# Expert tiles in a pinned order, gathers several tiles ahead, and one gathered row per expert in layer 2

## The chip, the cores and the metric

The kernel runs on one core of a Trainium2 chip, as one launch. The metric is the device time of a run in microseconds; lower is better. A core has five engines with their own instruction streams: PE (TensorE, matrix products into PSUM), DVE (VectorE), ACT (ScalarE), POOL (GpSimd) and SP (SyncE). SP and ACT issue plain DMAs, POOL issues the gathers by index. An engine works through its own stream in order and waits on semaphores for the others.

## The reference

Four layers work on x of 8 sequences with 256 tokens of 256 numbers (2048 tokens in all). Each layer is a cross attention with 16 heads of 16 on ctx_1024, then a feed-forward block, each behind a layer norm and added to x with a gate:

```python
x = x + tanh(g_xattn[i]) * xattn_i(layernorm(x), ctx_1024)
x = x + tanh(g_ffn[i])   * ffn_i(layernorm(x))
```

Layers 1 and 2 have a mixture of experts as their feed-forward block, and the change is about these. Each token picks 2 of 8 experts; hidden size H is 1024 in layer 1 and 512 in layer 2:

```python
w, ind = top_k(x_flat @ Wr, 2)             # 2 of 8 experts per token
w = softmax(w, axis=-1)
# for each expert e, with ce its weight per token (0 where it was not picked):
h = gelu(x_flat @ W1[e] + b1[e])           # [tokens, H]
out += ce[:, None] * (h @ W2[e] + b2[e])   # [tokens, 256]
```

Layer 2 normalises its tokens by their root mean square first and adds its own input again. Layer 0's feed-forward block is a plain one, layer 3's one with ternary weights and a convolution. All products of the experts are in float32.

## The kernel before

`moe(l, ...)` is run between two attention stages, once for layer 1 and once for layer 2. `route` (from line 773) finds the two experts of each token. `slots` (from line 813) sorts the 4096 pairs of token and expert by expert, each expert's share rounded up to whole tiles of 128: `NTL` = 39 tiles. It leaves two index tables: `toki`, which token stands in each row of each tile, and `wrow`, which rows of the weight tables a tile needs.

`experts` (from line 950) then works tile by tile. The 39 tiles are cut into `WSETS` = 3 runs of `PER` = 13 consecutive tiles. Each run has its own weight buffers ("a set"), and `order` takes one tile of each run in turn. Where a tile has the same expert as the tile before it in its run, `slots` has put an index out of bounds into `wrow`: the gather is still issued, but moves no weights (lines 869 to 879). Per tile j there are three steps:

- `fetch(j)`: three gathers on POOL (line 944): 128 token rows from `xd` into `xg`, then the first weights with b1 (`w1e`), then the second weights with b2 (`w2e`). The loop calls it two tiles ahead.
- `first(j)`: two transposes of the tokens (`ptg`, line 978), their copy into `xgT` on DVE (line 981, or 983 with the norm's weights), 16 products in layer 1 or 8 in layer 2 (`phg`, line 994), and as many Gelus on ACT (`hg`, line 1000).
- `second(j)`: 8 or 4 products of 256 columns (`yg`, line 1009), the sum with b2 on DVE (`ysb`, line 1014), and the write to `yd` in DRAM by SP (line 1015).

The loop runs `first(order[k])`, `second(order[k - 1])`, then pieces of the next stage whose place is at most k (`early`), then `fetch(order[k + 2])`. This order is not what the engines see: the tile framework orders each engine's stream itself, by priority and by its own estimate of when things are ready. Only instructions that were given to `pin` (line 132) keep their order among each other on their engine. `mm` and `turn` (lines 174 and 179) are pinned forms of a product and a transpose; the attention stages use them. The expert products before the change were not pinned.

`early` holds work of the next attention stage that needs no tokens: `setup(l)` (weights and bias of that layer), and the K and V projections of its first two jobs (`EARLY` = 2; a job is one sequence of one layer). Each job has four such steps, `proj("k", 0)`, `proj("k", 1)`, `vals(0)` and `vals(1)`, and `stack` cuts K into three bf16 parts, writes them to DRAM (`dr_k`) and reads them back in seven row groups by six DMAs into `kstack`, all on SP. In layer 2's stage `early` also holds the ternary weights of layer 3 (sums on DVE, `wsum` on PE).

After the stage, `element(b)` of `experts` gathers the results of a sequence (`yg<-yd`, four gathers on POOL per sequence) and adds them to x on DVE (line 1047). Then the attention's `norm` (with a pow on POOL, line 154), `normT` and the Q projection follow.

`ones_of` (line 198) fills what is constant in a K stack and a V buffer: rows 96 to 127 of the stack are set to 1 (rows 112 to 114 are used so, the others are overwritten), and the V buffer gets its column of ones. The stacks of jobs 0 and 1 live through the whole kernel, the third belongs to each attention's own pool and is filled anew in each of the three runs, by POOL (line 199).

Of the kernel before, what the change touches and what calls it, by code (L numbers as in the profile page):

```python
# [8 lines left out]
F32 = mybir.dt.float32  # L9
BF16 = mybir.dt.bfloat16  # L10
I32 = mybir.dt.int32
AF = mybir.ActivationFunctionType
ALU = mybir.AluOpType
AX = mybir.AxisListType

P = 128
B, S, D = 8, 256, 256
# [3 lines left out]
DC = D // P  # L21
# [3 lines left out]
NE = 8  # L25
NTL = 2 * T // P + NE - 1
NEG = -(2.0**100)
WSETS = 3
PER = -(-NTL // WSETS)
EARLY = 2  # L30
# [8 lines left out]
def kernel(ctx: ExitStack, tc: tile.TileContext, a: dict, out: bass.AP):  # L39
# [157 lines left out]

    def ones_of(engine, ks, va):
        engine.memset(ks[96:P], 1.0)
        engine.memset(va[:, :, :, DK : DK + 1], 1.0)  # L200
        engine.memset(va[:, :, :, DK + 1 :], 0.0)

    def attention(layers):
# [61 lines left out]
        def prep(j, l, b):  # L265
# [4 lines left out]
            def begin():  # L270
                if j < 3 and (j >= EARLY or l == 0):
                    ones_of(nc.vector if j < EARLY else nc.gpsimd, stacks["k"][j], vas[j])
                o["nm"] = pool.tile([P, 2, NH], F32, tag="nm", name=f"nm_{n}", bufs=3)

            def context():
# [105 lines left out]
            def vals(i):  # L381
# [9 lines left out]
                )  # L391

            if l == 0:
                return [
                    (-3, begin), (-3, context), (-2, norm), (3, normT), (4, contextT), (5, biasT),
                    (6, contextV),
                ]
# [4 lines left out]
            if j < EARLY:  # L402
                early.extend([(NTL - 11 + 4 * j + i, f) for i, (_, f) in enumerate(kv)])
                kv = []
            return [
                (-6, begin), (-5, norm), (0, normT),
# [405 lines left out]

    def slots(l, pool, scratch, one1, one2):

# [33 lines left out]
        while k < NE:  # L848
# [6 lines left out]

        n = WSETS * PER
        ge = tmp("ge", [P, n, NE])
# [10 lines left out]

        ts = te.rearrange("p (w i) -> p w i", w=WSETS)
        same = tmp("same", [P, WSETS, PER - 1])  # L870
        nc.vector.tensor_tensor(same, ts[:, :, 1:], ts[:, :, : PER - 1], ALU.is_equal)
        wr = tmp("wr", [P, n])
        nc.vector.tensor_copy(wr, te)
        nc.vector.scalar_tensor_tensor(
            wr.rearrange("p (w i) -> p w i", w=WSETS)[:, :, 1:], same, float(NE * P),
            ts[:, :, 1:], ALU.mult, ALU.add,
# [72 lines left out]

    def experts(l, pool, xd, chosen, rows, nh, scale, early):  # L950
        one1, one2, wa, wb = chosen
        toki, wrow, s1, s2 = rows
        yd = dram.tile([NTL * P, D], F32, name=f"yd{l}")
        n1 = DC * nh * P
        xg, w1, w2, hs = {}, {}, {}, {}
        wsets = [
            (
                pool.tile([P, n1 + nh], F32, tag=f"w1e{k}", name=f"w1e{l}_{k}", bufs=1),
                pool.tile([P, nh * D + D], F32, tag=f"w2e{k}", name=f"w2e{l}_{k}", bufs=1),
            )  # L960
            for k in range(WSETS)
        ]

        def fetch(j):
            xg[j] = pool.tile([P, D], F32, tag="xg", name=f"xg{l}_{j}", bufs=4)
            gather(xg[j], xd[:, :], toki[:, j : j + 1])
            w1[j], w2[j] = wsets[j // PER]
            for w, n in ((w1[j], "a"), (w2[j], "b")):
                gather(
                    w, a[f"L{l}_ffn_w{n}"], wrow[:, j : j + 1],  # L970
                    bounds_check=NE * P - 1, oob_is_err=False,
                )

        def first(j):
            pv = bank(ps_m, "m", f"ptg{l}_{j}")[:, : DC * P].rearrange("p (c s) -> p c s", c=DC)
            x_ = xg.pop(j)
            for c in range(DC):
                nc.tensor.transpose(pv[:, c, :], x_[:, c * P : (c + 1) * P], ident)
            xT = pool.tile([P, DC, P], F32, tag="xgT", name=f"xgT{l}_{j}", bufs=2)
            if scale is None:  # L980
                nc.vector.tensor_copy(xT, pv)
            else:
                nc.vector.tensor_tensor(
                    xT, pv, scale[:, :, None].to_broadcast([P, DC, P]), ALU.mult
                )
            h = pool.tile([P, nh, P], F32, tag="hg", name=f"hg{l}_{j}", bufs=2)
            w = w1[j]
            for g in range(nh // 4):
                ph = bank(ps_s, "s", f"phg{l}_{j}_{g}").rearrange("p (k s) -> p k s", k=4)
                for k in range(4):  # L990
                    hc = 4 * g + k
                    for c in range(DC):
                        lo = c * nh * P + hc * P
                        nc.tensor.matmul(  # L994
                            ph[:, k, :], lhsT=w[:, lo : lo + P], rhs=xT[:, c, :],
                            start=(c == 0), stop=(c == DC - 1),
                        )
                for k in range(4):
                    hc = 4 * g + k
                    nc.scalar.activation(  # L1000
                        h[:, hc, :], ph[:, k, :], AF.Gelu, bias=w[:, n1 + hc : n1 + hc + 1]
                    )
            hs[j] = h

        def second(j):
            py = bank(ps_t, "t", f"yg{l}_{j}")[:, :D]
            h = hs.pop(j)
            for hc in range(nh):
                nc.tensor.matmul(  # L1009
                    py, lhsT=h[:, hc, :], rhs=w2[j][:, hc * D : (hc + 1) * D],  # L1010
                    start=(hc == 0), stop=(hc == nh - 1),
                )
            ys = pool.tile([P, D], F32, tag="ysb", name=f"ysb{l}_{j}", bufs=3)
            nc.vector.tensor_tensor(ys, py, w2[j][:, nh * D :], ALU.add)  # L1014
            nc.sync.dma_start(yd[j * P : (j + 1) * P, :], ys)

        order = [
            j for i in range(PER) for j in range(i, WSETS * PER, PER) if j < NTL
        ]
        for j in order[:2]:  # L1020
            fetch(j)

        early = sorted(early, key=lambda q: q[0])
        for k in range(NTL + 1):
            if k < NTL:
                first(order[k])
            if k:
                second(order[k - 1])
            while early and early[0][0] <= k:
                early.pop(0)[1]()  # L1030
            if k + 2 < NTL:
                fetch(order[k + 2])

        def element(b):
            rows = [
                (t, s, w) for t in (2 * b, 2 * b + 1) for s, w in ((s1, wa), (s2, wb))
            ]
            g = []

            def fetched(pool):  # L1040
                for k, (t, s, w) in enumerate(rows):
                    g.append(pool.tile([P, D], F32, tag="yg", name=f"yg{l}_{b}_{k}", bufs=4))
                    gather(g[k], yd[:, :], s[:, t : t + 1])

            def added(pool):
                for k, (t, s, w) in enumerate(rows):
                    pin(nc.vector.scalar_tensor_tensor(
                        x[t], g[k], w[:, t, :], x[t], ALU.mult, ALU.add
                    ))

            at = NH * (b - 2) - AHEAD
            return [(at - 16, fetched), (at - 7, added)]

        return [q for b in range(B) for q in element(b)]
# [209 lines left out]

    def moe(l, nh, lg, xd, gate, early, scale=None):
        with tc.tile_pool(name=f"c{l}", bufs=1) as pool:
            with tc.tile_pool(name=f"rt{l}", bufs=1) as tmp:
                chosen = route(pool, tmp, lg, gate, l)
                rows = slots(l, pool, tmp, chosen[0], chosen[1])
            with tc.tile_pool(name=f"f{l}", bufs=1) as tiles:  # L1270
                return experts(l, tiles, xd, chosen, rows, nh, scale, early)

# [6 lines left out]
    early, run = attention((2,))  # L1279
    ahead = moe(1, 8, lg[0], xd[0], tg[:, 5:6], early)  # L1280
    with tc.tile_pool(name="r2", bufs=2) as pool:
# [3 lines left out]
    with tc.tile_pool(name="f3w", bufs=1) as home:  # L1285
        weights, pieces = ffn3(home)
        ahead = moe(2, 4, lg[1], xd[1], tg[:, 6:7], early + weights, w["nw"])
        with tc.tile_pool(name="r3", bufs=2) as pool:
            run(pool, pieces(pool), ahead)


def _layout(inputs):
# [43 lines left out]
    for l, w1, w2 in (  # L1336
# [5 lines left out]
        b1 = g[f"L{l}_ffn_b1"].reshape(NE, -1, P).transpose(0, 2, 1).reshape(NE * P, -1)  # L1342
        r[f"L{l}_ffn_wa"] = np.concatenate([first, b1], axis=1)

        second = w2.reshape(NE, -1, P, D).transpose(0, 2, 1, 3).reshape(NE * P, -1)
        b2 = np.repeat(g[f"L{l}_ffn_b2"], P, axis=0)
        r[f"L{l}_ffn_wb"] = np.concatenate([second, b2], axis=1)
    r["L3_ffn_w1"], r["L3_ffn_w2"] = g["L3_ffn_w1"].T, g["L3_ffn_w2"].T
# [26 lines left out]
```

## Time and profile before

| | us |
|---|---|
| median of 3 runs | 1856.42 (1855.35 to 1860.22) |
| profiled execution | 1884.49, its span 1882.7 |
| layer 1's expert stage, first gather to last output | 624.8 to 925.0 |
| layer 2's expert stage, first gather to last output | 1233.8 to 1434.3 |

The profile shows one execution. Busy times in it count an engine's instructions; a product in float32 has two records on PE and two on PEld (loading of the stationary operand). A row of the timeline has the start, the length, the engine, the line, the operation and the tiles it writes and reads; what stands in brackets is how long the engine had been idle and what ended that. "issue" there means that the profile shows no cause. The kernel has 27329 instructions, of which PE has 9856 products; PE is busy in 77% of the span, DVE in 49%, ACT in 39%, POOL in 38%. The mean granted clock of PE is 0.893 of full speed.

### The profile page before, as it was taken

How to read it: one execution, taken by the hardware profiler on the slowest of the kernel's cores; microseconds unless marked ns; L12 is line 12 of the kernel's file. 1: busy time of each engine (PE TensorE's matmuls, PEld its weight loads, DVE VectorE, ACT ScalarE, POOL GpSimd, SP SyncE). 2: the span in 40 equal slices, each digit the busy share in tenths (PEclk: the TensorE clock that was granted, in tenths of full speed). 3: DMA queues.
4: the chain of work that ended last, by engine and by line, in shares of the span. 5: the costliest groups of instructions: out<-in, count | busy, mean ns of one | idle time of the engine just before them, and what ended most of it. 6: DMA issues, size and time to landing. Idle time of an engine off the chain costs nothing.

```text
span 1882.7 us, 27329 instructions
## 1 busy us (share of the span) xinstructions
PE 1447.0 (77%) x9856; PEld 1093.2 (58%) x9886; DVE 921.1 (49%) x2642; ACT 739.8 (39%) x1623; POOL 723.5 (38%) x849
## 2 busy tenths in 40 slices
PE   1598898989996699999658978458885667667753
PEld 1366666766664599999635655347784345444422
DVE  5655554345564210112155676522222557778877
ACT  0255454545553133233214545112221246555641
POOL 4342322232310433434344541055654534544352
PEclk9999999999997799999868999779997688888876
DMA  8653222324440432325236443133443452222000
GB/s 213 136 125 73 63 57 57 75 67 86 110 100 29 168 107 68 124 88 148 69 87 133 118 101 82 62 113 103 133 129 79 103 106 68 68 63 67 9 6 17
DMA packets 101981, 170.02 MB, mean 90 GB/s; under 512 B 30355, under 2 KB 84502, under 8 KB 92118
## 3 DMA queue, kind: packets, MB, share of 16 engines
q1 hardware_dynamic: 68096, 114.33, 24.8%
q0 software_dynamic: 29280, 52.83, 10.0%
q10 hardware_dynamic: 4470, 1.10, 0.3%
q8 instruction: 79, 1.29, 0.3%
q14 instruction: 56, 0.46, 0.1%
HBM read 224.69 MB, written 41.68 MB: 141 GB/s over the span
## 4 chain that ended last, share of the span: by engine, by line
PE 52%; DVE 16%; DMA 10%; issue 10%; POOL 7%; ACT 3%; SPq 1%; ACTq 0%; POOLq 0%; another core or an unknown queue 0%; DVEq 0%
PE yg L1009 10%; PE phg L994 10%; PE y_f L175 4%; PE po L175 4%; PE ph_f L175 4%; PE st L175 3%; PE sc L175 3%; PE pq L175 3%; DMA kstack<-dr_k 3%; DMA qstack<-dr_q 3%; PE pk L175 2%; DVE nm L432 2%; PE pv L175 2%; DVE h_f L1188 1%; DVE ms L427 1%
## 5 line engine op out<-in xcount | busy, mean ns | idle before, releaser
L476 ACT ACTIVATE pT<-st 128x512 f32<-128x512 f32 x512 | 298.4, 597 | 288.8 <-PE st L175 232.5
L432 DVE TENSOR_REDUCE nm<-sc 128x2 f32<-128x512 f32 x384 | 257.2, 684 | 152.6 <-PE sc L175 151.1
L175 PE MATMUL sc<-kstack,qstack 112*128 112x256 bf16 x1024 | 214.4, 295 | 115.5 <-DMA kstack<-dr_k 25.8
L1000 ACT ACTIVATE hg<-phg,w1e 128x128 f32<-128x128 f32 x468 | 133.8, 369 | 308.2 <-issue 230.3
L1009 PE MATMUL yg<-w2e,hg 128*128 128x256 f32 x936 | 228.9, 386 | 24.3 <-ACT hg L1000 14.4
L994 PEld LDWEIGHTS phg<-xgT,w1e 128*128 128x128 f32 x1872 | 225.3, 196 | 14.1 <-issue 7.9
L994 PE MATMUL phg<-xgT,w1e 128*128 128x128 f32 x1872 | 227.3, 279 | 7.2 <-DMA w1e<-in_L_ffn_wa,sl_wrow 5.6
L175 PE MATMUL st<-qstack,kstack 115*128 115x256 bf16 x1024 | 208.0, 288 | 29.5 <-ACT pT L476 26.8
L175 PEld LDWEIGHTS <-qstack 112*128 112x128 bf16 x1024 | 100.8, 104 | 185.7 <-issue 108.4
L1009 PEld LDWEIGHTS yg<-w2e,hg 128*128 128x128 f32 x936 | 169.2, 192 | 49.0 <-ACT hg L1000 19.9
L1014 DVE TENSOR_TENSOR ysb<-yg,w2e 128x256 f32<-128x256 f32 x78 | 33.1, 424 | 328.1 <-PE yg L1009 297.3
L175 PE MATMUL po<-pT,va 128*32 128x256 f32 x2048 | 151.5, 413 | 0.9
L427 DVE CUSTOM_DVE_ANT_0 ms<-sc,mb 128x256 f32<-128x256 f32 x256 | 107.5, 420 | 77.9 <-PE sc L175 67.7
L944 POOL DMA_INDIRECT w2e<-in_L_ffn_wb,sl_wrow x78 | 77.3, 991 | 163.7 <-DVE ysb L1014 155.9
L175 PEld LDWEIGHTS <-kstack 115*128 115x128 bf16 x1024 | 104.5, 103 | 56.6 <-issue 37.3
L154 POOL TENSOR_TENSOR rsr_ff<-rsv_ff,nhalf 128x4 f32<-128x4 f32 (+2 forms) x24 | 24.4, 1017 | 227.4 <-DVE rsv_ff L152 123.9
L944 POOL DMA_INDIRECT xg<-xd,sl_toki x78 | 77.1, 988 | 89.5 <-DVE sl_toki L940 65.9
L944 POOL DMA_INDIRECT w1e<-in_L_ffn_wa,sl_wrow x78 | 77.5, 993 | 54.3 <-ACT hg L1000 32.7
L944 POOL DMA_INDIRECT yg<-yd,sl_si x64 | 62.8, 981 | 81.9 <-issue 39.6
L175 PEld LDWEIGHTS po<-pT,va 128*32 128x32 f32 x2048 | 56.5, 114 | 60.9 <-issue 37.7
L184 POOL CAST pc_q<-qT 128x512 bf16<-128x512 f32 x22 | 14.4, 654 | 176.0 <-ACT qT L371 133.1
L180 PE MATMUL px<-ident,xn 128*128 128x128 f32 x128 | 26.9, 346 | 68.9 <-DVE xn L330 68.7
(253 smaller groups left out, 2486.8 us busy)
## 6 DMA issues: line engine op xcount, KB each, us to landing
kstack<-dr_k SPq DMA_DIRECT2D x160, 128.0 KB
qstack<-dr_q SPq DMA_DIRECT2D x64, 256.0 KB
dr_q<-pc_q SPq DMA_DIRECT2D x32, 384.0 KB
dr_k<-pc_k SPq DMA_DIRECT2D x32, 384.0 KB
qstack<-dr_q SPq DMA_DIRECT2D x32, 384.0 KB
yd<-ysb SPq DMA_DIRECT2D x78, 128.0 KB
kstack<-dr_k SPq DMA_DIRECT2D x32, 256.0 KB
xd<-fxn_f SPq DMA_DIRECT2D x8, 512.0 KB
```

Source lines behind the costliest of these rows:

```text
L154: nc.gpsimd.tensor_tensor(rs, ve, nhalf[:, :k, :n], ALU.pow)
L175: pin(nc.tensor.matmul(out, lhsT=lhsT, rhs=rhs, start=start, stop=stop, skip_group_check=True))
L180: pin(nc.tensor.transpose(out, in_, idn))
L427: nc.vector.tensor_tensor_reduce(masked, sc[:, i, :], o["bias"][:, i, :], -1.0, 3.0e38, ALU.add, ALU.min, o["nm"][:, i, h : h + 1],)
L432: nm = nc.vector.tensor_reduce(o["nm"][:, :, h], sc, AX.X, ALU.max, negate=True)
L476: pin(nc.scalar.activation(pT[u], st, AF.Exp))
L944: return nc.gpsimd.indirect_dma_start(out=dst, out_offset=None, in_=src, in_offset=bass.IndirectOffsetOnAxis(ap=rows, axis=0), **kw,)
L994: nc.tensor.matmul(ph[:, k, :], lhsT=w[:, lo : lo + P], rhs=xT[:, c, :], start=(c == 0), stop=(c == DC - 1),)
L1000: nc.scalar.activation(h[:, hc, :], ph[:, k, :], AF.Gelu, bias=w[:, n1 + hc : n1 + hc + 1])
L1009: nc.tensor.matmul(py, lhsT=h[:, hc, :], rhs=w2[j][:, hc * D : (hc + 1) * D], start=(hc == 0), stop=(hc == nh - 1),)
L1014: nc.vector.tensor_tensor(ys, py, w2[j][:, nh * D :], ALU.add)
L1188: nc.vector.scalar_tensor_tensor(y, hp[:, k, t : t + S], cw[:, hc, t : t + 1], y, ALU.mult, ALU.add)
```

## The change

The expert stage is rewritten:

- Transposes and products go through `turn` and `mm`, and the gathers of tokens and weights through `pin`. PE's order is then that of the program: products of tile k, transposes of tile k+1, second products of tile k-1.
- Tokens are gathered four tiles ahead (five buffers instead of four). The weights of the next tile of the same set are gathered as soon as the code has passed the last use of the buffer: in layer 1 the first weights behind `first(k)`, the second behind `second(k - 1)`; in layer 2 both in one gather behind `second(k - 1)`.
- Layer 1 keeps three sets and two gathers per tile (`apart`). Layer 2 gets five sets, and its four weight parts lie in one row of one table (2308 numbers), fetched by one gather per tile. The table is laid out on the host as before.
- The early K and V projections: those of job 0 are placed at k = 32 to 35 (28 to 31 before), those of job 1 all at k = 39, behind the last tile (32 to 35 before).
- The third K stack is no longer filled by a memset on POOL: a DMA on SP copies the three rows of ones out of job 0's stack. The V buffer's memsets stay on POOL.

```diff
+            def ones_own():
+
+                nc.sync.dma_start(stacks["k"][j][NR : NR + 3], kkeep[0][NR : NR + 3])
+                ones_of(nc.gpsimd, vas[j])
...
+            own = [(0, ones_own)] if j == EARLY else []
...
-                early.extend([(NTL - 11 + 4 * j + i, f) for i, (_, f) in enumerate(kv)])
+                early.extend([(NTL - 7 + i if j == 0 else NTL, f) for i, (_, f) in enumerate(kv)])
...
-        n = WSETS * PER
+        per = -(-NTL // nsets)
+        n = nsets * per
...
-    def experts(l, pool, xd, chosen, rows, nh, scale, early):
+    def experts(l, pool, xd, chosen, rows, nh, scale, early, nsets, apart):
...
+        cuts = [(0, n1), (n1, n1 + n2)] if apart else [(0, n1 + n2)]
...
+        def tokens(k):
+            if k < NTL:
+                j = order[k]
+                xg[j] = pool.tile([P, D], F32, tag="xg", name=f"xg{l}_{j}", bufs=5)
+                pin(gather(xg[j], xd[:, :], toki[:, j : j + 1]))
+
+        def weights(k, part):
+
+            if k < NTL and part < len(cuts):
+                j = order[k]
+                lo, hi = cuts[part]
+                pin(gather(
+                    wsets[j // per][:, lo:hi], a[f"L{l}_ffn_w{'ab'[part] if apart else ''}"],
+                    wrow[:, j : j + 1], bounds_check=NE * P - 1, oob_is_err=False,
+                ))
+
+        def turns(k):
...
-                nc.tensor.transpose(pv[:, c, :], x_[:, c * P : (c + 1) * P], ident)
+                turn(pv[:, c, :], x_[:, c * P : (c + 1) * P], ident)
...
-                        nc.tensor.matmul(
-                            ph[:, k, :], lhsT=w[:, lo : lo + P], rhs=xT[:, c, :],
-                            start=(c == 0), stop=(c == DC - 1),
-                        )
+                        mm(ph[:, k, :], w[:, lo : lo + P], xT[:, c, :], c == 0, c == DC - 1)
...
-                nc.tensor.matmul(
-                    py, lhsT=h[:, hc, :], rhs=w2[j][:, hc * D : (hc + 1) * D],
-                    start=(hc == 0), stop=(hc == nh - 1),
-                )
+                mm(py, h[:, hc, :], w[:, hc * D : (hc + 1) * D], hc == 0, hc == nh - 1)
...
-        for j in order[:2]:
-            fetch(j)
+
+        AHEADX = 4
+        for k in range(AHEADX):
+            tokens(k)
+            if k < nsets:
+                weights(k, 0)
+                weights(k, 1)
+        for k in range(AHEADX, nsets):
+            weights(k, 0)
+        turns(0)
 
         early = sorted(early, key=lambda q: q[0])
         for k in range(NTL + 1):
             if k < NTL:
-                first(order[k])
+                first(k)
+            turns(k + 1)
+            if apart and k < NTL:
+                weights(k + nsets, 0)
             if k:
-                second(order[k - 1])
+                second(k - 1)
+                weights(k - 1 + nsets, len(cuts) - 1)
+            tokens(k + AHEADX)
             while early and early[0][0] <= k:
                 early.pop(0)[1]()
-            if k + 2 < NTL:
-                fetch(order[k + 2])
...
-    ahead = moe(1, 8, lg[0], xd[0], tg[:, 5:6], early)
+    ahead = moe(1, 8, 3, True, lg[0], xd[0], tg[:, 5:6], early)
...
-        ahead = moe(2, 4, lg[1], xd[1], tg[:, 6:7], early + weights, w["nw"])
+        ahead = moe(2, 4, 5, False, lg[1], xd[1], tg[:, 6:7], early + weights, w["nw"])
```

## The prediction

> **What bounds the kernel now.** I read the page first. The chain that ended last runs over two product lines of the expert stages, L1009 and L994, each about 10% of the span, and holds 10% of "issue", time in which an engine waited for nothing that the profile shows.
>
> ```profile
> PE 52%; DVE 16%; DMA 10%; issue 10%; POOL 7%; ACT 3%; SPq 1%; ACTq 0%; POOLq 0%; another core or an unknown queue 0%; DVEq 0%
> ```
>
> So I next put the busy times of the engines against windows of the two expert stages. Columns: window and its length, busy time of PE, PEld, DVE, ACT and POOL, granted clock, DMA share, GB/s.
>
> ```profile
> 632.00:924.60 292.60, 292.51 (x1982) 271.59 (x1982) 34.71 (x86) 93.42 (x321) 110.20 (x112) 0.99 0.38 116
> 1239.60:1433.90 194.30, 168.33 (x1054) 149.57 (x1054) 45.70 (x114) 49.17 (x165) 111.29 (x113) 0.96 0.44 123
> 1383.26:1401.65 18.39, 18.39 (x122) 16.94 (x121) 5.62 (x12) 6.27 (x22) 12.32 (x12) 1.00 0.63 151
> 924.60:938.70 14.10, 0.00 (x0) 0.00 (x0) 4.37 (x12) 0.00 (x0) 9.37 (x8) 0.66 0.19 56
> 1433.90:1448.00 14.10, 0.02 (x1) 0.05 (x1) 4.53 (x12) 0.00 (x0) 9.44 (x8) 0.63 0.19 56
> ```
>
> The reader is to see three things. Layer 1's stage (first row, 39 tiles) has PE busy in 292.51 of 292.60 us: it is bound by PE's own work, and an order or an earlier gather can give nothing there. Layer 2's stage (second row) has 26 us without PE, although 18 us in it (third row) show the same work without a gap. And behind each stage PE stands still for 14 us, while DVE and POOL carry tokens back (last rows).
>
> Then layer 2's waits, from 1236 to 1436 us: who waited for what, us, times, longest.
>
> ```profile
> ACT hg L1000 <- issue: 109.6, 30, 7.4
> ...
> DVE xgT L983 <- PE ptg L978: 34.2, 18, 5.7
> ...
> POOL w2e L944 <- DVE ysb L1014: 28.6, 22, 3.6
> PEld yg L1009 <- ACT hg L1000: 19.7, 14, 4.6
> POOL w1e L944 <- ACT hg L1000: 15.4, 10, 2.9
> PE yg L1009 <- ACT hg L1000: 14.4, 12, 4.3
> ```
>
> It is a ring: PE's second product waits for the Gelu, POOL's weight gathers wait for Gelu and for the output of the tile that last used the set, and the token gather that PE needs next stands behind them. The timeline shows both forms, an ordinary tile and the worst stall:
>
> ```profile
> 1302.62 1.95 PE L994 MATMUL phg<-xgT,w1e 128*128 128x128 f32 x16
> 1304.41 0.38 PE L978 MATMUL ptg<-ident,xg 128*128 128x128 f32 x2
> 1304.66 1.15 ACT L1000 ACTIVATE hg<-phg,w1e 128x128 f32<-128x128 f32 x4 [3.14 <-issue]
> 1305.08 1.99 PE L1009 MATMUL yg<-w2e,hg 128*128 128x256 f32 x8 [0.29 <-issue]
> ...
> 1268.97 0.96 POOL L944 DMA_INDIRECT xg<-xd,sl_toki  x1 [0.30 <-issue]
> 1271.27 0.42 DVE L983 TENSOR_TENSOR xgT<-ptg,nw 128x256 f32<-128x256 f32 x1 [5.37 <-remote]
> 1271.28 1.14 ACT L1000 ACTIVATE hg<-phg,w1e 128x128 f32<-128x128 f32 x4 [7.40 <-issue]
> 1271.70 3.78 PE L1009 MATMUL yg<-w2e,hg 128*128 128x256 f32 x8 [4.32 <-ACT hg L1000]
> ```
>
> In layer 2 PE runs first product, next tile's transposes, then the second product of the same tile, which has to wait for its own Gelu: 4.28 us from tile to tile (1300.79 to 1305.08). In the stall the token gather left POOL at 1268.97, about 2.3 us before DVE and ACT went on: the tokens were late. The second product after it took 3.78 us instead of 1.99: after the pause PE is slow as well.
>
> **The change part by part.** All against this profiled execution, 1884.49 us (span 1882.7, 1.8 around it). It is 28.1 us above the median of 1856.42; I take the difference over unscaled, since the terms are PE work or waits on it.
>
> *Layer 2's order and gathers.* A tile's PE work is read from the dense window: there a tile with one early projection (4 records of pk or pv) takes 4.60 us, the projection 0.87, so a tile 3.73. In the new order first(k), turns(k+1), second(k-1), the Gelu of tile k has 0.22 (transposes) + 1.73 (second product) + 1.79 + 0.22 us before it is needed and takes 1.14 plus start; DVE's xgT (0.42) has 1.73. Both are covered. If that cover went, 0.55 us per tile would come back.
> Sum: start of the first product +1.5 (below); its cold clock, 3.65 instead of 1.79 now, stays: 1.9; 39 x 3.73 = 145.5; pgb and the two wsum 1.9; four projections of job 0 at 0.87: 3.5; last tile's tail 0.3. From 1239.6 + 1.5 that ends at 1394.2, where the last second product now ends at 1433.9: **-39.7**.
>
> *Start with one gathered row.* The first product now waits only for w1e: issued 1235.10, used 1239.60, 4.50 us for 0.53 MB; layer 1's for 1.05 MB took 5.71 (626.34 to 632.05). That is 1.2 us per 0.53 MB, so the combined row (1.18 MB) gives 4.50 + 1.5. Bounds 0 (longer rows move faster, see below) and 3; I take 1.5.
>
> *Five sets at the start, and a rule against it.* Each of the first five tiles needs a new set of 1.18 MB with tokens of 0.13 MB, in 3.73 us.
>
> ```profile
> 636.00:645.00 9.00, 9.00 (x65) 8.35 (x64) 0.85 (x2) 4.36 (x13) 4.30 (x5) 1.00 1.02 426
> 1240.00:1250.00 10.00, 7.74 (x45) 7.01 (x45) 1.00 (x3) 3.13 (x8) 5.90 (x6) 0.85 0.90 310
> ```
>
> Layer 1, whose rows have 8 to 9 KB, drew 426 GB/s; layer 2 with its rows of 4 to 5 KB 310. At 426 a set with tokens takes 3.1 us, at 310 it takes 4.2. The Trainium skill ("DMA: Bandwidth & Descriptors", Where 436 GB/s comes from) says that HBM to SBUF is held to about 358 GB/s per core by the HBM side: 3.7 us, no margin. By the rule or by the small-row rate four tiles would be late by 0 to 0.5 us each, 2 us at most; the new row has 9.2 KB, so the row of layer 1 is nearest and beats the rule: 0.
>
> *Later sets and tokens in one queue.* weights(k+4) is issued behind second(k-1), three tiles (11.2 us) before its use; 1.18 MB need about 6. Its tokens follow, used 7.4 us later; a token gather needs 3 us (1233.76 to 1236.73) and up to 2.8 more behind a set. Covered, unless two sets come in a row. The trace doesn't show the pinned order in layer 2; bounds: 0, as layer 1 shows, and the 14 us that all gaps over 0.9 us after the first tiles now hold. From 1380 to 1434, where layer 2 was densest, gaps of 1.18, 0.41 and 1.81 are left: I take **+3**. POOL issues 2 gathers at 0.98 with 0.30 between, 2.6 us a tile instead of 3.9, below 3.73.
>
> *Layer 1.* Same PE work, no wait to win: 0. Tile 1's w1 lands at about 637.6 by the DMA packets, when PE gets there: 0, at most +2.
>
> *Projections of job 1 moved behind the last tile.* In both layers 4 x 0.87 us leave PE's bound stretch and go into the 14 us hole. Layer 2's is in the sum already; layer 1 gives **-3.5**. With them move two ACT copies of K (0.47) and of V (0.37), DVE's split (0.46+0.69+0.43+0.69 = 2.3 us, done 4.6 after the last product, before the first token sum at +6.5) and seven DMAs on SP: dr_k, then six kstack, which wait for dr_k's landing. The last yd stands ahead of them on SP; the next SP work, dr_q, comes 23 us after the stage's end; K is used after qstack, 34 us. Cover is there; for DMA contention with the gathers of yg: between 0 and +1 each, **+1** in all.
>
> *The ones of the third stack.* POOL's memset goes, SP gets one DMA of 24 KB (0.4 us to issue, needed two elements later).
>
> ```profile
> 1441.97 3.51 POOL L199 MEMSET kstack<- 32x4096 bf16 x1
> ```
>
> It stands among the token gathers after each stage. The pow behind it was ready to start (DVE's rsv_a) at 1445.51 and began at 1446.66; at the first stage 936.27 and 937.43. So at most -1.2 each, and 0 if gathers fill the place: **-1** in all. At the kernel's start it had covered waits for weights: 0. The slot table grows from 39 to 40 columns: nothing.
>
> Sum: -39.7 + 3 - 3.5 + 1 - 1 = -40.2. Profiled 1844.3, median **1816**.
>
> **Rivals.**
> *Partial.* The Gelu wait goes (about 26 tiles x 0.55 = 14 us, and 7 from job 1's projections), but expert changes still stall PE as now. For: each of the long gaps lies near POOL's gathers. Against: tokens go from two tiles ahead to four. About -25: 1831.
> *The change doesn't do what it says.* If the late ACT and DVE starts were PE's own (its records show no wait, only "issue"), the order gives nothing, and 7 us from job 1's projections remain: 1849. Against: layer 1 runs the same instructions without a gap.
> *Slower: a set that is late stops everything.* With the order pinned, PE can't run second(k-1) or an early projection while first(k) waits for its row, and now the whole row counts, not w1 alone. Place: the up to seven expert changes in layer 2. It costs from the point where a set lands more than 10.7 us after issue; at 15 us it takes 4 of stall and 1.9 of cold clock, seven times, 41 us, the whole gain. At 19 us it would be 69: 1885. Against: 1.18 MB in about 6 us; two sets in a row 9.
>
> **How the numbers follow.** Chances: main case 0.73, its own range 1806 to 1825 (lead-in, residual gaps, tail); partial 0.14; order without effect 0.07; late sets 0.06. The range 1804 to 1836 takes in the first two. A measurement here tells 0.3% (5.6 us) from no change. Faster by more than that: main, partial and most of the third, 0.92; within: 0.03; slower: 0.05.
>
> **What would show it.** Layer 2's stage about 154 us long with PE busy in over 97%; tile to tile 3.73; "ACT hg <- issue" no longer followed by a waiting second product; POOL with two gathers per tile; pk and pv of job 1 after the last yg; layer 1's stage 289 us. Wrong: PE gaps of 3 us or more before phg at expert changes, a first product later than 1242 on today's time line, or a hole behind the stages longer than 14 us by more than 2.

## The result and the profile after

The changed kernel takes 1850.60 us (median of 15 runs, 1846.06 to 1856.78); beside it the kernel before took 1858.95 us (15 runs, 1853.80 to 1866.99). The ratio is 0.9954, 95% interval 0.9939 to 0.9969: 8.4 us faster, where 40 were forecast. The profiled execution of the changed kernel took 1846.81 us, its span is 1845.0.

First the windows of the changed kernel: layer 1's stage, the hole of PE behind it, layer 2's stage, its hole. Columns as before: window and length, busy time of PE, PEld, DVE, ACT and POOL, granted clock, DMA share, GB/s.

```profile
629.60:920.10 290.50, 289.98 (x1967) 272.62 (x1968) 35.28 (x81) 91.71 (x317) 109.41 (x112) 0.99 0.35 112
920.10:934.76 14.66, 3.99 (x17) 2.52 (x15) 6.39 (x16) 1.49 (x4) 8.93 (x11) 0.81 0.59 139
1234.37:1390.19 155.82, 155.30 (x1039) 145.74 (x1040) 43.82 (x109) 47.47 (x161) 71.29 (x73) 0.97 0.44 139
1390.19:1413.10 22.91, 3.99 (x18) 2.53 (x16) 6.45 (x17) 1.69 (x4) 9.07 (x15) 0.64 0.51 114
```

Layer 2's stage is now as dense as layer 1's: PE is busy in 155.30 of 155.82 us. But the hole behind it has grown from 14.1 to 22.9 us, while layer 1's kept its 14.7. The 4 us of PE work in both are the moved projections.

The waits of the changed kernel from 1232 to 1392 us, a few of the rows:

```profile
ACT hg L1020 <- issue: 87.9, 33, 4.3
DVE xgT L1002 <- PE ptg L178: 63.4, 33, 7.5
POOL we L950 <- DVE ysb L1033: 51.6, 30, 6.1
...
PE phg L173 <- DMA we<-in_L_ffn_w,sl_wrow: 3.7, 1, 3.7
```

The row "PE yg <- ACT hg", 14.4 us in 12 waits in the profile before, is gone. ACT still has a large "issue" row, but no product waits behind it. PE's one wait for weights is the first, ahead of the stage. The timeline shows one tile:

```profile
1289.87 1.95 PE L173 MATMUL phg<-xgT,we 128*128 128x128 f32 x16
...
1290.76 0.99 POOL L950 DMA_INDIRECT we<-in_L_ffn_w,sl_wrow  x1 [1.48 <-DVE ysb L1033]
...
1291.65 0.38 PE L178 MATMUL ptg<-ident,xg 128*128 128x128 f32 x2
...
1291.87 1.89 PE L173 MATMUL yg<-we,hg 128*128 128x256 f32 x8
1291.90 1.14 ACT L1020 ACTIVATE hg<-phg,we 128x128 f32<-128x128 f32 x4 [2.59 <-issue]
...
1293.60 1.95 PE L173 MATMUL phg<-xgT,we 128*128 128x128 f32 x16
```

From first product to first product 3.73 us (1289.87 to 1293.60). The Gelu of the tile starts with the second product of the tile before it, and is done long before its own. The tail of layer 2's stage shows the new hole:

```profile
1386.57 3.62 PE L173 MATMUL yg<-we,hg 128*128 128x256 f32 x16
...
1392.79 0.47 ACT L375 ACTIVATE kT<-pk,bk 128x256 f32<-128x256 f32 x1 [1.22 <-PE pk L173]
1393.29 0.43 DVE L182 CAST pc_k<-kT 128x512 bf16<-128x512 f32 x1 [7.88 <-ACT kT L375]
...
1394.94 0.69 DVE L185 TENSOR_TENSOR pc_k<-res_k,pc_k 128x512 bf16<-128x512 f32 x1
...
1395.55 0.74 DVE L1033 TENSOR_TENSOR ysb<-yg,we 128x256 f32<-128x256 f32 x2
1395.66 0.37 SPq L248 DMA_DIRECT2D dr_k<-pc_k  x1
1396.12 1.07 SPq L1034 DMA_DIRECT2D yd<-ysb  x2
1398.27 2.63 SPq L256 DMA_DIRECT2D kstack<-dr_k  x6
1399.68 0.97 POOL L950 DMA_INDIRECT yg<-yd,sl_si  x1 [24.66 <-DMA yd<-ysb]
...
1406.34 0.48 DVE L1074 SCALAR_TENSOR_TENSOR x<-yg,rt_wa,x 128x256 f32<-128x256 f32 x1 [10.04 <-issue]
```

The last products end by 1390.19. DVE stands idle for 7.88 us in front of the split of K, which waits for the moved projections, and only behind the split come the sums of the last two tiles (1395.55), though their products are long done. SP sends `dr_k` ahead of the last two `yd`. So POOL's first gather of results leaves at 1399.68, 9.49 us after the last product, and its rows reach the sum 6.66 us later, beside the six DMAs of `kstack`. In the profile before, the last product ended at 1433.87, and these two rows followed:

```profile
1437.19 0.97 POOL L944 DMA_INDIRECT yg<-yd,sl_si  x1 [13.52 <-issue]
...
1440.18 0.48 DVE L1047 SCALAR_TENSOR_TENSOR x<-yg,rt_wa,x 128x256 f32<-128x256 f32 x1 [5.86 <-DMA yg<-yd,sl_si]
```

There the two steps took 3.32 and 2.99 us. The gather is now late by 6.2 and slow by 3.7, less 1.0 that is won from the first sum to the next transposes `px` (7.8 us before, 6.8 now): the 8.8 us of the hole.

### The profile page after: what moved, and what is told of

Read it like the earlier page. It is cut to its first block, busy times and chain, and to the rows that moved or that the text cites. A ratio compares the mean times of both kernels' runs of the same rounds, so it can differ in the third digit from the quotient of the medians.

```text
span 1845.0 us, 27174 instructions
## 1 busy us (share of the span) xinstructions
PE 1440.9 (78%) x9886; PEld 1094.5 (59%) x9886; DVE 921.5 (50%) x2642; ACT 741.0 (40%) x1623; POOL 672.9 (36%) x807
## 3 DMA queue, kind: packets, MB, share of 16 engines
q8 instruction: 78, 1.28, 0.3%
## 5 line engine op out<-in xcount | busy, mean ns | idle before, releaser
L1020 ACT ACTIVATE hg<-phg,we 128x128 f32<-128x128 f32 x468 | 133.4, 368 | 271.4 <-issue 223.6
L173 PE MATMUL phg<-xgT,we 128*128 128x128 f32 x1872 | 228.7, 280 | 8.0 <-DMA we<-in_L_ffn_w,sl_wrow 3.7
L173 PEld LDWEIGHTS phg<-xgT,we 128*128 128x128 f32 x1872 | 226.8, 196 | 13.7 <-issue 8.1
L173 PE MATMUL yg<-we,hg 128*128 128x256 f32 x936 | 214.7, 379 | 0.0
L173 PEld LDWEIGHTS yg<-we,hg 128*128 128x128 f32 x936 | 172.1, 190 | 20.2
L1033 DVE TENSOR_TENSOR ysb<-yg,we 128x256 f32<-128x256 f32 x78 | 33.0, 424 | 166.5 <-PE yg L173 162.2
L1000 DVE COPY xgT<-ptg 128x256 f32<-128x256 f32 x39 | 16.5, 424 | 139.9 <-PE ptg L178 139.9
L173 PE MATMUL pq<-xs,wq 128*128 128x256 f32 x192 | 73.3, 520 | 3.9 <-ACT qT L375 1.7
```

The costliest lines, as they stand in the source:

```text
L173: pin(nc.tensor.matmul(out, lhsT=lhsT, rhs=rhs, start=start, stop=stop, skip_group_check=True))
L1020: nc.scalar.activation(h[:, hc, :], ph[:, k, :], AF.Gelu, bias=w[:, n1 - nh + hc : n1 - nh + hc + 1],)
L1033: nc.vector.tensor_tensor(ys, py, w[:, nh * D :], ALU.add)
```

## The experiments

**The kernel before, unchanged, profiled again, twice.** No edit. The forecast had been worked out from one execution that lay 28.1 us above the median of its kernel.

> The kernel before, unchanged, for a second profile. Theory A (the one profiled execution of before was not typical: layer 2's expert stage drew out to 194 us by chance, and an ordinary run has it at about 168 us, because the ring of POOL, ACT and PE closes differently from run to run): the span of this profile is 1852 to 1865 us, layer 2's stage (first phg to last yg) 165 to 175 us, everything else within 3 us of the first profile. Theory B (profiling itself draws the stage out, timed runs don't see it): the span is near 1883 again and the stage near 194, with a timed ratio of 1.000. Rival C (the 38 us are real in the stage, and the changed kernel loses 28 us elsewhere in its timed runs): the span is near 1883 and so are the times; the 15 runs of before speak against it.

> The kernel before, unchanged, a third profiled execution. Theory (the first profiled execution of it, 1882.7 us, was the exception): layer 2's stage from the first phg to the last yg takes about 172 to 174 us with tiles of 4.28 us, PE's gaps in it are below 12 us, the span is about 1858 to 1862. Rival (the two are two ordinary ways for this kernel to run): the stage is again near 190 with irregular tiles.

Times 1861.58 us against 1860.57 beside it (ratio 1.0001, 0.9987 to 1.0015), and 1860.13 in the single third run. Layer 2's stage and its hole in the second profiled execution of this kernel:

```profile
1240.10:1412.80 172.70, 163.34 (x1054) 146.28 (x1054) 45.80 (x114) 49.15 (x165) 111.32 (x113) 0.99 0.49 138
1412.80:1426.90 14.10, 0.00 (x1) 0.03 (x1) 4.53 (x12) 0.00 (x0) 9.40 (x8) 0.69 0.19 56
```

And layer 2's stage in the third:

```profile
1239.01:1412.23 173.22, 163.19 (x1054) 146.13 (x1054) 45.61 (x114) 49.16 (x165) 111.47 (x113) 0.99 0.50 138
```

172.7 and 173.2 us, against 194.3 in the execution that the forecast was made from. That one was the exception, by 21.6 us, three quarters of the 28 by which it lay above the median. None of some 90 timed runs of this kernel, those beside the other versions included, took more than 1868.44 us. One ordinary tile of the second execution:

```profile
1291.35 1.99 PE L1009 MATMUL yg<-w2e,hg 128*128 128x256 f32 x8 [0.29 <-ACT hg L1000]
...
1295.22 1.14 ACT L1000 ACTIVATE hg<-phg,w1e 128x128 f32<-128x128 f32 x4 [3.14 <-issue]
...
1295.64 1.99 PE L1009 MATMUL yg<-w2e,hg 128*128 128x256 f32 x8 [0.29 <-ACT hg L1000]
```

The tile takes 4.29 us (1291.35 to 1295.64) with the wait for its own Gelu, as the forecast had it; what is missing are the long stalls. The waits of this execution from 1236 to 1413 us show how often the ring closes:

```profile
PE yg L1009 <- ACT hg L1000: 7.5, 21, 1.4
```

It does in 21 of the 39 tiles, which at 0.55 us is about 12 us. So what the change could win was these 12 us and the moved projections; the stage became 16.9 us shorter (172.70 to 155.82), and not 38.

**The order alone.** The kernel before, with its transposes split off from `first` and all its expert products pinned; fetches, sets, tables and projections as they were.

```diff
-                nc.tensor.transpose(pv[:, c, :], x_[:, c * P : (c + 1) * P], ident)
+                turn(pv[:, c, :], x_[:, c * P : (c + 1) * P], ident)
...
+        turns(order[0])
...
             if k < NTL:
                 first(order[k])
+            if k + 1 < NTL:
+                turns(order[k + 1])
```

> The kernel before with the pinned order of the products and transposes alone (first(k), turns(k+1), second(k-1)); gathers still two tiles ahead, three sets, two weight gathers, early projections and memset as before. If the order carries layer 2's gain (Gelu wait gone, 0.55 us per tile): layer 2's stage about 15 us shorter than in e1, ratio about 0.992. If the order pays only with gathers further ahead: the stage has PE gaps at the transposes or at phg of 1 us and more and is no shorter than in e1, ratio 1.000 or above.

1859.45 us, ratio 1.0001 (0.9987 to 1.0016): nothing. Layer 2's stage in the windows of this kernel:

```profile
1234.05:1405.15 171.10, 159.39 (x1054) 146.51 (x1054) 46.27 (x114) 49.15 (x165) 111.86 (x113) 0.99 0.50 140
```

Its ordinary tiles take 3.73 us, but PE now stands in 11.7 us (171.10 less 159.39), and its waits from 1232 to 1405 us say for what:

```profile
PE ptg L180 <- DMA xg<-xd,sl_toki: 6.5, 7, 1.8
...
PE phg L175 <- DMA w1e<-in_L_ffn_wa,sl_wrow: 6.4, 5, 2.0
```

Tokens and weights that were in time for a PE that waited for the Gelu are late for one that doesn't. The wait has changed its place.

**The gathers without the order.** The changed kernel, its expert products and transposes not pinned.

```diff
-                        mm(ph[:, k, :], w[:, lo : lo + P], xT[:, c, :], c == 0, c == DC - 1)
+                        nc.tensor.matmul(
+                            ph[:, k, :], lhsT=w[:, lo : lo + P], rhs=xT[:, c, :],
+                            start=(c == 0), stop=(c == DC - 1),
+                        )
...
-                turn(pv[:, c, :], x_[:, c * P : (c + 1) * P], ident)
+                nc.tensor.transpose(pv[:, c, :], x_[:, c * P : (c + 1) * P], ident)
```

> The changed kernel with its expert products and transposes unpinned, all else as changed (gathers pinned and ahead, five sets, one row, projections late). If the gathers carry the gain and the order nothing: ratio as the changed kernel's, 0.995. If the order is needed: layer 2's stage shows the 4.28 us tile with its Gelu wait again, 10 to 15 us longer than the changed kernel's 155 us, ratio 1.000 to 1.003.

1867.76 us, ratio 1.0040 (1.0026 to 1.0053), slower than the kernel before. Layer 2's stage takes 172.70 us, and the Gelu is back in its waits (1240 to 1414 us):

```profile
PEld yg L1034 <- ACT hg L1023: 18.0, 28, 1.8
...
PE yg L1034 <- ACT hg L1023: 8.7, 15, 1.4
```

Its hole is 23.01 us, as in the changed kernel: the hole has nothing to do with the pinned products. By itself the order brings 1.6 to 2.1 us of layer 2's stage (171.10 us against 172.70 and 173.22). The gathers, with the row and the sets, bring none: the stage is as long as before, although job 1's projections have left it.

**Job 1's projections where they were.** The changed kernel with one line as before.

```diff
-                early.extend([(NTL - 7 + i if j == 0 else NTL, f) for i, (_, f) in enumerate(kv)])
+                early.extend([(NTL - 11 + 4 * j + i, f) for i, (_, f) in enumerate(kv)])
```

> The changed kernel with the early projections where they were (job 0 at 28 to 31, job 1 at 32 to 35). In the changed kernel's profile the last two ysb of layer 2 stood behind job 1's split on DVE (1395.55 instead of about 1390.4), and the hole from the last yg to px grew from 14 to 23 us. If that is a real cost: layer 2's hole is back at 14 us, PE's stage 3.5 us longer in each layer, and the ratio to before is lower than the changed kernel's 0.9954 by 2 to 5 us (0.993 to 0.995). If the hole is as long from something else: ratio 0.997 to 0.999 (7 us of PE work back in the stages).

1851.49 us, ratio 0.9943 (0.9922 to 0.9964), not to be told from the changed kernel. Layer 2's stage is longer by 4.6 us and its hole shorter by 8.0:

```profile
1247.27:1407.73 160.46, 158.88 (x1054) 148.44 (x1054) 46.56 (x114) 49.14 (x165) 71.12 (x72) 0.97 0.46 143
1407.73:1422.62 14.89, 0.00 (x0) 0.03 (x1) 4.22 (x12) 0.00 (x0) 9.26 (x16) 0.68 0.27 81
```

Layer 1's stage is 293.0 us, 2.5 longer. Moving the projections won 7 us in the two stages and gave 8 back in one hole. And with the projections where they were, order and gathers together still bring 12 to 13 us of layer 2's stage (172.70 and 173.22 to 160.46).

**The tail pinned too.** The changed kernel; the sum `ysb` and DVE's split of the early jobs keep the order of the program, so the last results go first.

```diff
-    def split(dst, src, tmp, engine):
+    def split(dst, src, tmp, engine, keep_=lambda ins: ins):
-        engine.tensor_copy(dst[0], src)
+        keep_(engine.tensor_copy(dst[0], src))
...
+                pin if pool is None else lambda ins: ins,
...
-            nc.vector.tensor_tensor(ys, py, w[:, nh * D :], ALU.add)
+            pin(nc.vector.tensor_tensor(ys, py, w[:, nh * D :], ALU.add))
```

> The changed kernel with two more pins: the add of the tail (ysb) and the four DVE operations of the split of K and V are kept in program order, so that DVE has the last two ysb ahead of the split and SP the last two yd ahead of the transfers of the split. Theory (behind layer 2 the DVE and SP orders put the split, which waits for K's transposes, ahead of the last two tiles' results): the hole of PE between the last yg and the next px falls from 22.9 to 14 to 16 us, layer 2's stage stays at 155.8, the time is 7 to 8 us lower than the changed kernel's: about 1843, ratio 0.991. Rival (the moved projections of K and V themselves, beside the tail, make the hole): it stays above 20 us, ratio 0.995.

1839.37 us, ratio 0.9886 (0.9858 to 0.9914); the interval lies wholly below that of the changed kernel. Layer 2's stage and hole, in the windows of this version:

```profile
1234.56:1390.46 155.90, 155.38 (x1039) 145.81 (x1040) 44.15 (x110) 47.47 (x161) 71.89 (x73) 0.97 0.45 140
1390.46:1405.01 14.55, 3.99 (x18) 2.53 (x16) 6.39 (x16) 1.69 (x4) 9.03 (x15) 0.73 0.61 138
```

In its timeline the last sum now starts 0.04 us after the last product, and the split comes behind it:

```profile
1390.50 0.42 DVE L1034 TENSOR_TENSOR ysb<-yg,we 128x256 f32<-128x256 f32 x1 [1.30 <-PE yg L173]
...
1393.47 0.97 POOL L951 DMA_INDIRECT yg<-yd,sl_si  x1 [18.18 <-DMA yd<-ysb]
1393.57 0.43 DVE L182 CAST pc_k<-kT 128x512 bf16<-128x512 f32 x1 [2.64 <-ACT kT L376]
...
1396.46 0.48 DVE L1075 SCALAR_TENSOR_TENSOR x<-yg,rt_wa,x 128x256 f32<-128x256 f32 x1 [0.53 <-DMA yg<-yd,sl_si]
```

The gather leaves 3.0 us after the last product and lands in 2.99, and with the same projections in it the hole is 0.45 us longer than before the change (14.10). The profile is 9.9 us shorter than the changed kernel's (span 1835.1 against 1845.0), of which the hole is 8.4. The median is the lowest of all versions that were run.

Without these pins the order of the tail is the framework's, and it came out both ways. The split stands ahead of the last sums in the changed kernel, in the version without pinned products and in the one with three sets and two gathers (holes of 22.9, 23.0 and 24.1 us). In the next version it stands behind them (last sum at 1434.35, split at 1437.42), and there the hole is 14.8 us with the same projections in it.

**Three sets, one row.** The changed kernel, layer 2 with three weight sets.

```diff
-        ahead = moe(2, 4, 5, False, lg[1], xd[1], tg[:, 6:7], early + weights, w["nw"])
+        ahead = moe(2, 4, 3, False, lg[1], xd[1], tg[:, 6:7], early + weights, w["nw"])
```

> The changed kernel with three weight sets instead of five in layer 2, still one gathered row a tile. Theory (with three sets a fetch of weights for a tile can start only when the tile three earlier is done, too late for a row that takes about 6 us to land): layer 2's stage is 165 to 180 us, with waits of PE's phg for the weights' queue, time 1855 to 1868, ratio 1.00 to 1.005. Rival (the sets are more than needed and order and early issue do it all): the stage stays at 156, ratio 0.995.

1883.06 us, ratio 1.0118 (1.0085 to 1.0151); layer 2's stage 192.9 us, worse than I expected. Of its waits from 1240 to 1434 us:

```profile
PE phg L173 <- DMA we<-in_L_ffn_w,sl_wrow: 29.4, 10, 4.1
```

Ten waits of 2.9 us, the first of them ahead of the stage. The timeline has one of them:

```profile
1316.69 1.00 POOL L950 DMA_INDIRECT we<-in_L_ffn_w,sl_wrow  x1 [1.47 <-DVE ysb L1033]
...
1322.93 2.47 PE L173 MATMUL phg<-xgT,we 128*128 128x128 f32 x10 [3.13 <-DMA we<-in_L_ffn_w,sl_wrow]
```

Issued at 1316.69, used 6.24 us later: the row needs about 6 us, and with three sets the schedule leaves it about 2.8 (first product every 3.73 us, the gather 0.9 us into the tile before the one that needs it). The longer waits then cost again in PE's clock. Behind the six waits of 3.08 to 4.07 us inside the stage, the first products of a tile took 2.81 to 3.75 us; behind the three of 0.67 to 2.86 us they took 2.02, near the 1.95 of a tile without a wait. Over the stage the same products take 166.8 us of PE's time instead of 155.3, at a granted clock of 0.92 instead of 0.97.

**Four sets, one row, tail pinned.** The version with the tail pinned, with `moe(2, 4, 4, False, ...)` for layer 2.

> The version with the tail pinned and one gathered row a tile in layer 2, four weight sets instead of five. Theory (a set comes free one second product earlier than with three, so its row has one tile, 3.7 us, more to land; about 7 us against a landing of about 6): stage 156 to 162 us, ratio 0.989 to 0.992. Rival (the row needs more than 7 us from issue to use): stage 165 to 180, ratio 0.994 to 1.002.

1845.53 us, ratio 0.9897 (0.9859 to 0.9935); layer 2's stage 155.89 us, PE busy in 155.37. One tile more, which leaves the row 6.6 us, is enough.

**Three sets, two gathers.** The changed kernel, layer 2 with `moe(2, 4, 3, True, ...)` and two tables, so order, early gathers and moved projections stay, and the row and the sets go.

> The changed kernel with three sets and two gathers a tile in layer 2 (a table for the first weights and one for the second, as before), the pinned order and the early issue kept. Theory (POOL issues three gathers of 1.29 us a tile, 3.9 us, just above PE's 3.73): layer 2's stage is 158 to 164 us, the lead from the first gather to the first phg back at 5.7 us, the time 3 to 6 us above the changed kernel's, ratio 0.997 to 0.999. Rival 1 (the row and the sets bring nothing beside order and early issue): stage 156, ratio 0.995. Rival 2 (they bring most of it): stage 170 or more, ratio 1.00 or above.

1851.48 us, ratio 0.9952 (0.9928 to 0.9976): the changed kernel's time. My theory fell and its first rival held: the single row and the two further sets bring nothing beside order and early gathers. Layer 2's stage:

```profile
1229.88:1386.06 156.18, 153.89 (x1039) 143.87 (x1040) 43.63 (x109) 47.61 (x161) 111.73 (x113) 0.98 0.50 144
```

POOL's 117 gathers of 1.29 us are 151 us, within the stage's 156, since the first of them come ahead of it; a stream that is four tiles ahead can be a little slower per tile. And with two gathers the program issues the first weights right behind the first product that used their part of the set, a tile earlier than the single row; this is the likely reason that three sets suffice. The lead, from the first gather to the first product, is back at 5.8 us from 7.3.

**The same, with the tail pinned.**

> The version with the tail pinned, and layer 2 back at three weight sets and two gathers a tile. Theory (five sets and the single row bring nothing beside order and early gathers, and cost 1.5 us of lead): hole behind layer 2 about 14.5 us, layer 2's stage 156, lead 5.8 instead of 7.2, time 0 to 2 us below the tail-pinned version's, ratio 0.987 to 0.989. Rival (the tie of the version with three sets and two gathers with the changed kernel was an accident of few runs, and the third gather of POOL costs): stage 158 or longer, ratio 0.990 or above.

1844.73 us, ratio 0.9896 (0.9872 to 0.9920). The stage (156.1), lead (5.8) and hole (14.6) came out as expected; the intervals of this version and of the one with five sets overlap, and which is faster is not settled.

**Tokens two tiles ahead.** The version just above, with one number changed (and the second weights of the third set gathered at the start).

```diff
-        AHEADX = 4
+        AHEADX = 2
...
             weights(k, 0)
+            weights(k, 1)
```

> The version of the run before this one (tail pinned, three sets, two gathers) with tokens gathered two tiles ahead instead of four in both layers; order and weight gathers unchanged. Theory (tokens two ahead stand behind weight gathers that wait for a set to come free, so transposes wait): layer 2's stage 162 to 172 us with PE waits at ptg, ratio 0.992 to 0.998. Rival (only the place of the weight gathers matters): stage 156 to 158, ratio 0.987 to 0.989.

2114.43 us, ratio 1.1332 (1.1299 to 1.1366), far beyond what either theory gave. Layer 1's stage goes from 289.8 to 398.5 us, layer 2's from 156.1 to 327.5. A tile of layer 1 in the timeline of this version:

```profile
784.70 3.73 PE L173 MATMUL phg<-xgT,we 128*128 128x128 f32 x32
784.90 0.42 DVE L1034 TENSOR_TENSOR ysb<-yg,we 128x256 f32<-128x256 f32 x1 [3.03 <-PE yg L173]
...
785.59 0.99 POOL L951 DMA_INDIRECT we<-in_L_ffn_wb,sl_wrow  x1 [3.71 <-DVE ysb L1034]
...
786.89 0.96 POOL L951 DMA_INDIRECT xg<-xd,sl_toki  x1 [0.30 <-issue]
...
789.79 0.41 PE L178 MATMUL ptg<-ident,xg 128*128 128x128 f32 x2 [1.36 <-DMA xg<-xd,sl_toki]
```

POOL's pinned stream has the tokens behind the second weights, these wait for `ysb`, `ysb` for the second product, and the transposes stand ahead of the next second product in PE's pinned stream. With two tiles ahead that is a closed ring: the tokens leave 2 us after `ysb` and are wanted before they land, in nearly every tile (in layer 2, 36 waits of 3.1 us for 39 tiles). The kernel before also fetched two ahead, but its fetch took the tokens ahead of the weights, and its gathers were not pinned. Both streams pinned, it is the four tiles that open the ring.

## Why the prediction was wrong, point by point

- **Baseline: the step that failed most.** "I take the difference over unscaled, since the terms are PE work or waits on it." The 28.1 us by which that execution lay above the median were not spread over it: 21.6 of them sat in layer 2's stage (194.3 us against 172.7 and 173.2), the very stage whose stalls I meant to remove. They are counted as gain in the -39.7. Set against that one execution, the changed kernel's profile is 37.7 us shorter (1882.7 to 1845.0), close to the forecast; set against the other two (1859.7 and 1858.3), it is 13 to 15.
- **The stall, misread.** "The tokens were late" was said of the start at 1271.27. The transposes that DVE waited for are recorded before that:

```profile
1266.99 0.38 PE L978 MATMUL ptg<-ident,xg 128*128 128x128 f32 x2
```

  Counted from the stage's start these are the seventh tile's, whose tokens left POOL at 1260.87. The gather that left at 1268.97 is the ninth, and its transposes are recorded at 1282.23. So the tokens were not late. DVE and ACT started within 0.01 us of each other, at 1271.27, on work that PE's records put before 1267.4. It looks as if PE finished late, but no record says so or says why. The cause stays open. Shown is only that the kernel also runs without the stall, by the two further executions.
- **Layer 2 after: right.** The ring was priced at "about 26 tiles x 0.55 = 14 us"; order and gathers without the moved projections bring 12 to 13. 39 tiles of 3.73 us; stage "about 154" (with the +3 for gaps 156), measured 155.8, PE busy in 99.7%. Lead +1.5, measured +1.6 (5.7 to 7.3). From the first profiled execution the stage and lead changed by -36.9, the sum had -36.7; from an ordinary one they changed by -15.3.
- **Five sets and the bandwidth rule: right to set it at 0.** From 1236 to 1246 us the changed kernel moved 384 GB/s. The Trainium skill ("DMA: Bandwidth & Descriptors", Where 436 GB/s comes from) has about 358 for this path; the measurement is above it, and PE has 0.5 us of gaps in the whole stage.
- **Late sets: the mechanism is real, but five sets keep clear of it.** Three sets show it (nine waits inside the stage, +37 us); with four the row has 6.6 us, with five a tile more, and it needs about 6.
- **Projections in the hole: "Cover is there", with +1 in all, was mis-sized, +9.3 measured** (hole 14.1 to 22.9 behind layer 2, 14.2 to 14.7 behind layer 1). I had "The last yd stands ahead of them on SP" from the program's text; the engines' streams are ordered by the tile framework, and behind layer 2 it put the split first. Shown by pinning those five instructions: 14.55 us. The prediction's own sign for this, a hole longer than 14 by more than 2, is what appeared.
- **Layer 1: -3.5 forecast, -2.3 measured** (292.8 to 290.5; the other versions with the same layer 1 have 289.6 to 289.9). Memset: -1 forecast, ahead of px; what was won there is part of the hole above. From px to the first scores behind the two holes 1.2 and 0.4 us were won against the second execution; whether the memset did that was not tried.

Taken together: 21.6 of baseline, 8.3 of hole and 1.2 of layer 1, less 0.6 for what was won behind px beyond the 1 forecast, make 30.5 of the 31.8 us between the forecast change (-40.2) and the measured one (-8.4). The rest is within the scatter: in three profiled executions of the kernel before, the first product of layer 1's stage starts at 629.2 to 632.1 us.

The forecast of "order without effect" (1849) is near the measured time, and is not what happened: the order works, where the gathers are early enough, and the tail gave half of it back. That the two numbers are close is chance.

## What to carry to other kernels

When the profiled execution lies above the median of the timed runs, find the stretch that holds the excess before working from it: look for irregular tiles and waits without a recorded cause, and price only the waits that recur in the ordinary tiles. A wait that is removed by pinning an order comes back at the next supplier unless that one is moved ahead in the same step; and where two pinned streams wait for each other, a late supplier can cost in every tile. Work that is moved into a hole has to be followed into every stream it enters, as the engine executes it and not as the program is written: an instruction that waits stands in front of the results that the hole is waiting for.

## What of the hardware was not expected

- One execution of the kernel before was 21.6 us longer in one stage, at a granted clock there of 0.96 instead of 0.99, with a pause of PE of 4.3 us whose cause the trace doesn't show.
- A gather of 128 result rows is in use 2.99 us after its issue starts, and took 6.66 beside the six row copies of `kstack` that were issued 1.4 us ahead of it; that these copies are the reason is an inference from their place, as in the tail-pinned version they come later.
- In these runs PE paid for a long pause twice, for a short one only once. In the run with tokens two ahead, layer 1's products, the same in number and shape, took 321.5 us of PE's time instead of 288.7 beside 77 us of gaps, at a granted clock of 0.92 instead of 0.99. Five tiles with pauses of 1.28 to 1.55 us, and then one behind a pause of 5.34 us:

```profile
754.49:798.59 44.10, 37.19 (x250) 34.31 (x251) 4.25 (x10) 11.44 (x40) 14.70 (x15) 1.00 0.18 55
811.36:822.89 11.53, 10.20 (x51) 8.86 (x51) 0.85 (x2) 2.29 (x8) 1.95 (x2) 0.76 0.08 23
```

  In the first stretch the clock was 1.00, and a tile's second products took 3.62 us, as in the version with tokens four ahead. Behind the long pause the clock was 0.76, and they took 6.17 us.
